# Four fused transformer layers on one core: the order of layer 0's first loads and keys, and unread products on constants in TensorE's waits

## The chip, the core and the metric

One core of a Trainium2 chip runs the whole program in one launch. The metric is device time in microseconds (us). Five engines work side by side, each through its own instructions in program order: TensorE (PE in the profile, with its weight loads as PEld), VectorE (DVE), ScalarE (ACT), GpSimd (POOL) and SyncE (SP, which only issues DMAs here; ACT issues some too, shown as ACTq).

## The reference

`x` has 1024 tokens of 128 features (16 batches of 64), `ctx_1024` as many. Four layers follow each other, all in float32:

```python
x = x + L0_xattn(ctx, ln(x), ...)   # 16 heads of 64; keys and values: ln(ctx) and ln(ln(x)), 128 a batch
x = x + L0_ffn(ln(x), ...)          # int8 weights, SiLU, 512 wide
x = x + L1_xattn(ln(x), ctx, ...)
x = x + L1_ffn(...)                 # mixture of 8 experts, two iterations
x = x + L2_xattn(ln(x), ctx, ctx, ...)   # 16 heads of 8, causal
x = x + L2_ffn(ln(x), ...)          # quantises by the largest |x| and the largest |hidden| of ALL tokens
x = x + L3_xattn(ln(x), ctx, ctx, ...)   # 16 heads of 8, scores outside a window raised by 1
x = x + L3_ffn(ln(x), ...)          # top 2 of 8 experts
```

In layer 0, with `A = Wq Wk^T / 8` and `N = Wv Wo` made for each head, scores are `(l A) kv^T` and the output is a sum over heads of `(softmax kv) N`. In layer 2's FFN the two maxima over all tokens are barriers: nothing behind one starts before every token has passed it.

## The kernel before, in words

**Layer 0** goes through eight pairs of batch groups `q` (four batches each). For each `q`, `l0_load` issues two DMAs into one `kv_tok` tile, the context rows from SP and the x rows from ACT. `l0_inputs` normalises it: `bn_stats` and `bn_aggr` (L154, L155), POOL's power (L161), four `tensor_scalar` (L183), a multiplication and an addition by `gains` (L403, L404; on DVE for q = 0, on POOL otherwise), four transposes on PE (L408), ACT's copy to `kvT` (L409), and two splits into float32r parts: `latT_hi` (L213) and `latT_lo` (L218) of the latent half, `tokp` of the tokens. `l0_project` then makes `G` (the latents times `A`) for eight pairs of heads, six products of 128x256 each (L236), copied by ACT (L425), and `l0_unit` has the scores (L445), the softmax on DVE, ACT and POOL (L447 to L461), the transposes (L465), the products with the tokens (L236) and with `N` (L479). Two `kv_tok` buffers take turns, so the load for `q + 2` waits until all readers of `q` are done. `l0_products` makes `A` and `N` (L326); `take_A` splits `A` into `A_hi` (ACT, L364) and `A_lo` (DVE, L365).

Units of layer 0 are interleaved, and one step of the tasks in `K.behind` (the weights and groups of the following sublayers) goes with each of them. A planner then puts the instructions of every engine into a final order by its own estimate of times, so a small edit can move instructions far from it. `in_turn` gives it an order between two instructions without a semaphore; `tc.issue_after` does the same for a block.

The order on SP at the start, as the source has it: `kv_tok` for q = 0, `WqT`, `gains`, `WqT`, `kv_tok` for q = 1, `WvT`, the four tiles of `x` (one for each group of four batches, first read when layer 0 adds its output), `cols` (every bias and small vector as columns), and then the weights of later layers. `later_constants` makes `half_cols` (half of `cols`, DVE L299), which ACT's sigmoid `sw` (L663) reads.

**Layers 2 and 3** have heads of 8 features. `heads_tile` goes through 16 tiles (group g, tile t): POOL lays out the keys (`kb`), PE adds a mask and the scores (L1262, L1263), DVE subtracts the maximum (L1264, L1265), ACT takes the exponential (L1266), PE transposes (L1273), ACT copies (`hpT`, L1274), PE multiplies by the values (L1283), DVE divides (L1291, L1292). `WARM` and `WARM_END` set how many unread products `keep_warm` puts behind the transposes of a tile: the weights are `identb` (a bf16 identity), what streams is a constant mask, and the output bank is never read. Before, this happens on the last two tiles of layer 3 (2, 4 and 2 products), sixteen times at the first queries of layer 2, and three times in layer 3's FFN for the groups g >= 2. `l2_ffn_hidden` has the two barriers, each through `global_amax`: a reduction on DVE, one product on PE (L1342), a reduction (L1344), four short steps (L1326 to L1331), and then the rounding of the tokens (`codes`, L1356 to L1359). `heads_keys` makes layer 3's keys on PE (L1137) and copies them with ACT (`hk`, L1147); part of it stands around the barriers.

Of the kernel before, what the change touches and what calls it, by code (L numbers as in the profile page):

```python
# [4 lines left out]


# [3 lines left out]

# [14 lines left out]
ALU = mybir.AluOpType  # L25
AX = mybir.AxisListType

P = 128
NT = 16
NG = 4  # L30
GT = 4
# [3 lines left out]
S = 64  # L35
EPS = 1e-5
NEG = -1.0e30
# [19 lines left out]
NCOL = sum(n for _, n in COLS)  # L57
# [150 lines left out]
def split(K, pool, src, name, engine=None, bufs=None, after=None):  # L208

    nc = K.nc  # L210
    hi = pool.tile(list(src.shape), F32R, name=f"{name}_hi", bufs=bufs)
    lo = pool.tile(list(src.shape), F32R, name=f"{name}_lo", bufs=bufs)
    first = nc.scalar.copy(hi, src) if isinstance(K, Later) else nc.vector.tensor_copy(hi, src)  # L213
    if after:
        in_turn(K, [after, first])
    if not isinstance(K, Later):
        K.mark = first
    (engine or nc.gpsimd).tensor_tensor(lo, src, hi.bitcast(F32), ALU.subtract)  # L218
    return hi, lo


# [61 lines left out]
def constants(K, pool):  # L283

    nc = K.nc
    K.ident = pool.tile([P, P], F32, name="ident")
    make_identity(nc, K.ident)
    K.neghalf = pool.tile([P, 1], F32, name="neghalf")
    nc.vector.memset(K.neghalf, -0.5)


def later_constants(K, pool):
    nc = K.nc
    K.identb = pool.tile([P, P], BF16, name="identb")
    nc.vector.tensor_copy(K.identb, K.ident)
# [3 lines left out]
    nc.vector.tensor_scalar(K.half, K.cols, 0.5, None, ALU.mult)  # L299

    K.pair_mask = pool.tile([P, GT, P], BF16, name="pair_mask")
    nc.vector.memset(K.pair_mask, NEG)
    for b in range(2):
        nc.vector.memset(K.pair_mask[b * S : (b + 1) * S, :, b * S : (b + 1) * S], 0.0)
# [11 lines left out]
N_TAGS = "2n"  # L316


def l0_products(K, out, left, right, hf, tags=("s", "t")):


    ps = [bank(K, tag, [P, 4, P]) for tag in tags]
    for j in range(4):
        for r in range(2):
            rows = slice(r * S, (r + 1) * S)
            K.nc.tensor.matmul(ps[r][:, j, :], left[rows, 4 * hf + j, :], right[rows, 4 * hf + j, :], start=True, stop=True)  # L326
    for r in range(2):
        out(ps[r], hf, r)


def l0_xattn(K):


    nc, tc, ins = K.nc, K.tc, K.ins
    with (
        tc.tile_pool(name="l0x_w", bufs=1, reuse_waits="tile") as wp,
        tc.tile_pool(name="l0x_g", bufs=2, reuse_waits="tile") as gp,
        tc.tile_pool(name="l0x_t", bufs=L0_BUFS, reuse_waits="tile") as tp,
    ):
        C = SimpleNamespace(gp=gp, tp=tp, tok={}, keys={}, G={})  # L340

        C.A = tuple(wp.tile([P, 16, P], F32R, name=f"A_{n}") for n in ("hi", "lo"))
        C.N = wp.tile([P, 16, P], F32, name="N")
        with tc.tile_pool(name="first", bufs=1, side="right", reuse_waits="tile") as first:
            l0_load(K, C, 0)
            w = {n: first.tile([P, 8, P], F32, name=n) for n in ("WqT", "WkT", "WvT", "Wo")}
            from_dram = {n: ins[f"L0_xattn_{n}"].rearrange("(c p) d -> p c d", p=P) for n in w}
            half = [slice(4 * hf, 4 * hf + 4) for hf in range(2)]
            gains = wp.tile([P, 2, P], F32, name="gains")
            K.kv_gamma, K.kv_beta = gains[:, 0, :], gains[:, 1, :]  # L350
            for hf in range(2):
                nc.sync.dma_start(w["WqT"][:, half[hf], :], from_dram["WqT"][:, half[hf], :])
                nc.scalar.dma_start(w["WkT"][:, half[hf], :], from_dram["WkT"][:, half[hf], :])
                if hf == 0:
                    nc.sync.dma_start(gains, ins["gains"])
            l0_load(K, C, 1)
            nc.sync.dma_start(w["WvT"], from_dram["WvT"])
            nc.scalar.dma_start(w["Wo"], from_dram["Wo"])
            heads = lambda t, hf, r: t.rearrange("p (c r) d -> p r c d", r=2)[:, r, half[hf], :]

            def take_A(ps, hf, r):
                hi, lo = (heads(a, hf, r) for a in C.A)
                scale = 1.0 / math.sqrt(64.0)
                nc.scalar.activation(hi, ps, AF.Copy, scale=scale)  # L364
                nc.vector.scalar_tensor_tensor(lo, ps, scale, hi.bitcast(F32), ALU.mult, ALU.subtract)  # L365

            l0_inputs(K, C, 0)
            for hf in range(2):
                l0_products(K, take_A, w["WqT"], w["WkT"], hf)
                for n in range(4 * hf, 4 * hf + 4):  # L370
                    l0_project(K, C, 0, n, "gn"[n % 2])
            l0_inputs(K, C, 1)

            with tc.issue_after(K.projected.ins):
                for hf in range(2):
                    l0_products(K, lambda ps, hf, r: nc.scalar.copy(heads(C.N, hf, r), ps), w["WvT"], w["Wo"], hf, N_TAGS)
        for g in range(NG):
            K.x[g] = K.load(K.const, f"x{g}", [P, GT, P], K.tokens(ins["x"], g))
        K.cols = K.load(K.const, "cols", [P, NCOL], ins["cols"])
        mid_begin(K)  # L380
        units = [(q, t, hf, b) for q in range(8) for t in range(2) for hf in range(2) for b in range(2)]
        interleave(K, (Task(l0_unit(K, C, *u)) for u in units), L0_DEPTH, L0_LAG, L0_RATE)


def l0_load(K, C, q):
    tok = C.tok[q] = C.gp.tile([P, GT, P], F32, name="kv_tok")
    for rows, name, queue in ((slice(0, S), "ctx_1024", K.nc.sync), (slice(S, P), "x", K.nc.scalar)):
        batches = K.ins[name].rearrange("(b s) d -> s b d", s=S)
        queue.dma_start(tok[rows, :, :], batches[:, GT * q : GT * (q + 1), :])


def l0_inputs(K, C, q):

    nc, gp = K.nc, C.gp
    tok = C.tok[q]
    mv = ln_moments(K, gp, tok)
    rs = gp.tile([P, GT], F32, name="ln_rs")
    nc.vector.tensor_scalar(rs[0:S, :], mv[0:S, :, 1], EPS, None, ALU.add)
    nc.vector.tensor_scalar(rs[S:P, :], mv[S:P, :, 1], 1.0 + EPS, EPS * EPS, ALU.mult, ALU.add)
# [5 lines left out]
    kvT = gp.tile(full, F32, name="kvT", bufs=3)  # L405
    ps = bank(K, "1", full)
    for b in range(GT):
        nc.tensor.transpose(ps[:, b, :], tok[:, b, :], K.ident)  # L408
    nc.scalar.copy(kvT, ps)  # L409
    latp = split(K, gp, kvT[:, :, S : 2 * S], "latT", nc.vector)  # L410
    tokp = split(K, gp, tok, "tokp", bufs=3)
    C.keys[q] = (kvT, latp, tokp)

# [14 lines left out]
def l0_unit(K, C, q, t, hf, b):  # L428
# [5 lines left out]
    G = C.G[q]  # L434
    if n == 0 and q + 2 < 8:
        l0_load(K, C, q + 2)
    if n == 2 and q + 2 < 8:
        l0_inputs(K, C, q + 2)
    if (hf, b) == (0, 0):
# [602 lines left out]
LAST_ENDS = ((2, 4), (2, 4))  # L1042
LAST_TAGS = "scgt"
HEAD_BLOCKS = ("L2", "L3")
WARM = ((0, 0, 0, 0), (0, 0, 2, 4))
WARM_END = 2


def heads_constants(K, pool):
# [185 lines left out]
def heads_tile(K, C, g, t):  # L1235
# [32 lines left out]
    pT = C.pp.tile([P, 8, P], F32, name="hpT")  # L1268
    for n in range(2):
        ps = bank(K, TURN[C.i], [P, 4, P])  # L1270
        for j in range(4):
            h = n * 8 + 2 * j
            turn = nc.tensor.transpose(ps[:, j, :], e[:, h : h + 2, :].rearrange("p h k -> p (h k)"), K.ident)  # L1273
        nc.scalar.copy(pT[:, n * 4 : n * 4 + 4, :], ps)  # L1274
    yield
    warm = WARM[C.i][t] if g == NG - 1 else 0
    if warm:
        keep_warm(K, bank(K, "s", [P, 512]), warm, turn)
    po = bank(K, AV[C.i][t % len(AV[C.i])], [P, 8, 2, 9])
# [21 lines left out]

    tiles = slice(t + 1 - n, t + 1)
    xg = K.x[g][:, tiles, :]
    if warm and t == GT - 1:
# [27 lines left out]
    return sc, inv  # L1332


def global_amax(K, pool, per_group, name):

    nc = K.nc
    one = pool.tile([P, 1], F32, name=f"{name}_one")
    nc.vector.tensor_reduce(one, per_group, AX.X, ALU.max)

    ps = bank(K, "g", [P, P])
    nc.tensor.matmul(ps, one.to_broadcast([P, P]), K.ident, start=True, stop=True)  # L1342
    out = pool.tile([P, 1], F32, name=f"{name}_all")
    nc.vector.tensor_reduce(out, ps, AX.X, ALU.max)  # L1344
    return out
# [22 lines left out]
def keep_warm(K, ps, n, after=None):  # L1368

    cols = ps.shape[-1]  # L1370
    moving = K.masks[1].rearrange("p h k -> p (h k)") if len(K.masks[1].shape) == 3 else K.masks[1]
    for _ in range(n):
        step = K.nc.tensor.matmul(ps, K.identb, moving[:, :cols], start=True, stop=True)
        if after is not None:
# [57 lines left out]
def l2_ffn_hidden(K, gp):  # L1432
    nc, wp = K.nc, K.l2p

    amax = global_amax(K, wp, K.l2am, "x")
    for xg in K.x:
        K.l2bo_step = nc.gpsimd.tensor_tensor(xg, xg, K.l2bo.unsqueeze(1).to_broadcast([P, GT, P]), ALU.add)
    sc, inv = scales(K, wp, amax, 1, 32767, "x")
# [10 lines left out]
    for g in range(NG):  # L1449
# [14 lines left out]
            if n == 1 or c % 2:  # L1464
                nc.vector.tensor_reduce(am[:, 4 * g + c : 4 * g + c + 1], h[:, c + 1 - n : c + 1, :], AX.XY, ALU.max, apply_absolute_value=True)
        K.l2h.append(h)
    amax = global_amax(K, wp, am, "h")
    sc, K.l2inv = scales(K, wp, amax, 1, 32767, "h")
    load_table(K, wp, AF.Exp, amax)
    steps = []  # L1470
# [48 lines left out]
def l3_ffn(K, gp, tp, g, tiles, tags):  # L1519
# [219 lines left out]
```

## Time and profile before

| | us |
|---|---|
| median of 3 runs (906.65 to 907.55) | 907.39 |
| the profiled execution, its own time | 907.62 |
| its span, first to last instruction | 905.9 |
| PE busy (share of the span) | 821.4 (91%) |
| DVE busy | 732.4 (81%) |
| ACT busy | 563.0 (62%) |
| POOL busy | 328.3 (36%) |

The span lies 1.7 us below the execution's own time. A busy share is an average over stages: in the first 17.9 us PE is busy for 5.25 us, from 30 to 310 us for 272.72 of 280 us. PEclk is the TensorE clock that the throttle granted; its mean is 0.98. The times of PE's instructions in one place against another tell the same thing for each instruction.

### The profile page before, as it was taken

The numbers are of one execution on the slowest core, as the hardware profiler recorded it, in microseconds if no ns is written. First come the engines' busy times: TensorE is split into PE (matmuls) and PEld (weight loads), VectorE is DVE, ScalarE is ACT, GpSimd is POOL, SyncE is SP. The second block draws the span as 40 slices with busy tenths as digits, with TensorE's granted clock in tenths as the row PEclk, the third lists the DMA queues.
The fourth block names the chain that finished last, engine by engine and source line by source line (L and its number), as shares of the span: only waits on it lengthen the run. The fifth ranks groups of instructions, "written<-read, shape, count | busy, mean of one in ns | idle before, by whom it ended". The sixth has DMA issues, their size and how long they took to land.

```text
span 905.9 us, 15766 instructions
## 1 busy us (share of the span) xinstructions
PE 821.4 (91%) x5859; PEld 671.2 (74%) x5868; DVE 732.4 (81%) x1877; ACT 563.0 (62%) x1093; POOL 328.3 (36%) x300
## 2 busy tenths in 40 slices
PE   4999999999999988899999799898999779898995
PEld 3989989979988876787787688684676447566663
DVE  5879799798698687877678877789788778789878
ACT  3676685676676599587687768564544484345443
POOL 3764574343243251511040310015474303435342
PEclk9999999999999999999999999999999999899998
DMA  8312000000000000000000000000000000000000
GB/s 191 106 36 59 13 2 12 13 1 1 13 1 1 1 13 0 15 14 21 1 1 1 1 1 1 0 25 1 1 2 1 1 1 1 1 1 1 13 13 24
DMA packets 22670, 13.73 MB, mean 15 GB/s; under 512 B 3009, under 2 KB 21953, under 8 KB 22593
## 3 DMA queue, kind: packets, MB, share of 16 engines
q1 hardware_dynamic: 18320, 10.62, 4.3%
q10 hardware_dynamic: 4272, 2.10, 0.9%
q8 instruction: 46, 0.75, 0.3%
q14 instruction: 32, 0.25, 0.1%
HBM read 11.66 MB, written 1.05 MB: 14 GB/s over the span
## 4 chain that ended last, share of the span: by engine, by line
PE 50%; DVE 25%; ACT 15%; POOL 3%; issue 3%; DMA 2%; SPq 1%; ACTq 0%; DVEq 0%; POOLq 0%
PE c_ps L918 7%; PE g_ps L479 4%; PE s_ps L1263 4%; PE s_ps L445 4%; PE g_ps L236 4%; PE c_ps L236 3%; PE g_ps L1283 2%; PE c_ps L1273 2%; PE s_ps L236 2%; PE t_ps L465 2%; PE t_ps L236 2%; ACT L941 2%; DVE mh_lo L895 1%; ACT L936 1%; DVE m L893 1%
## 5 line engine op out<-in xcount | busy, mean ns | idle before, releaser
L461 POOL TENSOR_TENSOR e<-e,rs 128x512 f32<-128x512 f32 x64 | 67.0, 1058 | 91.7 <-DVE rs L460 52.8
L161 POOL TENSOR_TENSOR ln_rstd<-ln_rs,neghalf 128x4 f32<-128x4 f32 (+1 forms) x38 | 40.8, 1073 | 144.8 <-DVE ln_rs L169 137.5
L1249 POOL TENSOR_TENSOR kb<-hk,head 128x1024 f32<-128x1024 f32 x32 | 63.7, 1993 | 74.2 <-PE s_ps L1263 58.9
L445 PE MATMUL s_ps<-kvT,G 128*128 128x128 f32 x512 | 71.7, 277 | 0.5 <-DVE e L451 0.5
L1263 PE MATMUL s_ps<-kb,hq 128*128 128x512 f32 x128 | 67.3, 609 | 2.1 <-ACT hq L1232 1.9
L445 PEld LDWEIGHTS s_ps<-kvT,G 128*128 128x128 f32 x512 | 65.8, 192 | 4.1 <-DVE e L451 1.9
L918 PE MATMUL c_ps<-mh_hi,w2e_hi 128*128 128x512 f32 x160 | 61.8, 426 | 4.5 <-ACT be L936 2.7
L479 PE MATMUL g_ps<-N,Ct 128*128 128x128 f32 x512 | 62.1, 276 | 1.1 <-ACT G L425 0.7
L479 PEld LDWEIGHTS g_ps<-N,Ct 128*128 128x128 f32 x512 | 60.1, 192 | 2.5 <-ACT G L425 1.3
L1266 ACT ACTIVATE e<-e 128x1024 f32<-128x1024 f32 x32 | 34.0, 1061 | 40.6 <-DVE e L1265 38.1
L1264 DVE TENSOR_REDUCE nm<-s_ps 128x8 f32<-128x512 f32 x64 | 43.7, 683 | 16.0 <-PE s_ps L1263 15.6
L1274 ACT COPY hpT<-c_ps 128x512 f32<-128x512 f32 x64 | 35.1, 589 | 34.2 <-PE c_ps L1273 33.9
L469 DVE TENSOR_TENSOR pT_lo<-t_ps,pT_hi 128x512 fp32r<-128x512 f32 x64 | 43.4, 683 | 13.5 <-ACT pT_hi L468 11.3
L918 PE MATMUL c_ps<-mh_hi,w2e_lo 128*128 128x512 f32 x160 | 51.9, 401 | 0.0
L895 DVE TENSOR_TENSOR mh_lo<-m,mh_hi 128x1024 fp32r<-128x1024 f32 x32 | 40.4, 1263 | 13.9 <-ACT mh_hi L894 12.9
L473 ACT COPY Ct<-c_ps 128x512 f32<-128x512 f32 x64 | 38.4, 600 | 21.2 <-PE c_ps L236 16.4
L918 PE MATMUL c_ps<-mh_lo,w2e_hi 128*128 128x512 f32 x160 | 49.4, 404 | 0.5 <-DVE mh_lo L895 0.5
L425 ACT COPY G<-g_ps 128x512 f32<-128x512 f32 x60 | 35.9, 598 | 21.4 <-PE g_ps L236 18.0
L452 ACT ACTIVATE e<-e 128x512 f32<-128x512 f32 x56 | 35.4, 638 | 20.8 <-DVE e L451 20.5
L1283 PEld LDWEIGHTS g_ps<-hv,hpT 128*64 128x64 f32 x1024 | 33.5, 137 | 19.3 <-issue 7.4
L447 DVE TENSOR_REDUCE nm<-s_ps 128x4 f32<-128x512 f32 x64 | 42.9, 679 | 5.0 <-PE s_ps L445 4.7
L468 ACT CAST pT_hi<-t_ps 128x512 fp32r<-128x512 f32 x64 | 38.1, 598 | 13.3 <-PE t_ps L465 7.3
(524 smaller groups left out, 2651.8 us busy)
## 6 DMA issues: line engine op xcount, KB each, us to landing
kv_tok<-in_x ACTq DMA_DIRECT2D x8, 128.0 KB, 3.3
kv_tok<-in_ctx SPq DMA_DIRECT2D x8, 128.0 KB, 2.9
x<-in_x SPq DMA_DIRECT2D x4, 256.0 KB, 8.3
ctx<-in_ctx SPq DMA_DIRECT2D x4, 256.0 KB, 3.4
w2e_raw<-in_L_ffn_expert_w SPq DMA_DIRECT2D x1, 768.0 KB, 4.4
out<-x SPq DMA_DIRECT2D x3, 256.0 KB, 2.3
WkT<-in_L_xattn_WkT ACTq DMA_DIRECT2D x2, 256.0 KB, 5.3
WqT<-in_L_xattn_WqT SPq DMA_DIRECT2D x2, 256.0 KB, 5.2
```

Source lines behind the costliest of these rows:

```text
L236: step = K.nc.tensor.matmul(ps, w[a], x[b], start=start and i == 0, stop=stop and i == 2)
L445: nc.tensor.matmul(ps[:, j, :], G[:, bb, h : h + 2, :].rearrange("p h s -> p (h s)"), kvT[:, bb, :], start=True, stop=True)
L447: K.mark = nc.vector.tensor_reduce(nm, ps, AX.X, ALU.max, negate=True)
L461: nc.gpsimd.tensor_tensor(e, e, rs.unsqueeze(2).to_broadcast([P, 4, P]), ALU.mult)
L469: nc.vector.tensor_tensor(lo, ps, hi.bitcast(F32), ALU.subtract)
L479: nc.tensor.matmul(ps, Ct[:, h, :], C.N[:, h, :], start=(h == 0), stop=(h == 15))
L895: nc.vector.tensor_tensor(lo, m, hi.bitcast(F32), ALU.subtract)
L918: nc.tensor.matmul(ps, K.w2p[part][:, 2 * n + i, cols], x[:, i, :, :], start=first, stop=last)
L1249: step = nc.gpsimd.tensor_tensor(kb, K.hk[C.i][g][:, :, t, :].unsqueeze(2).to_broadcast(full), K.head.unsqueeze(1).unsqueeze(3).to_broadca ...
L1263: nc.tensor.matmul(ps, hq[:, half, t, :, :].rearrange("p b s -> p (b s)"), kb[:, half, :, :], start=False, stop=True)
L1264: nc.vector.tensor_reduce(nm[:, heads], ps, AX.X, ALU.max, negate=True)
L1283: values = nc.tensor.matmul(po[b * S : (b + 1) * S, j, :, :].rearrange("p r d -> p (r d)"), pT[:, j, b * S : (b + 1) * S], K.hv[g][:, 2 * ...
```

## The change

At the start: `identb` and `pair_mask` are made first, eight unread products on them stand ahead of everything on PE, and six more behind the first half of `A`'s products. The second half of these products comes behind the transposes of q = 0. On DVE, the moments of q = 1 and `half_cols` come behind `latT_lo` of q = 0. On SP, `cols` moves ahead of `WvT`, and the four tiles of `x` move behind both loads for q = 2; the x rows of q = 2 are issued by SP in place of ACT. In the heads: unread products on the last two tiles of layer 2 (2, 4 and 2), on the first two of layer 3 (3 each), six ahead of the transposes of tile (2, 2) of layer 3, and three in layer 3's FFN of g = 1 as well. At the barriers: twelve behind the first maximum's product and five behind the second's. `keep_warm` streams `pair_mask` in place of layer 3's mask.

```diff
@@ split
-    (engine or nc.gpsimd).tensor_tensor(lo, src, hi.bitcast(F32), ALU.subtract)
+    K.split_end = (engine or nc.gpsimd).tensor_tensor(lo, src, hi.bitcast(F32), ALU.subtract)
@@ constants: identb and pair_mask are made here, no longer in later_constants
...
@@ later_constants
-    nc.vector.tensor_scalar(K.half, K.cols, 0.5, None, ALU.mult)
+    in_turn(K, [K.lat0, nc.vector.tensor_scalar(K.half, K.cols, 0.5, None, ALU.mult)])
@@ l0_products: with after=..., each product in_turn behind it
...
@@ l0_xattn
             l0_load(K, C, 0)
+            keep_warm(K, bank(K, "1", [P, 512]), WARM_START)
...
             l0_load(K, C, 1)
+            K.cols = K.load(K.const, "cols", [P, NCOL], ins["cols"])
             nc.sync.dma_start(w["WvT"], from_dram["WvT"])
...
+            step = l0_products(K, take_A, w["WqT"], w["WkT"], 0)
+            keep_warm(K, bank(K, "g", [P, 512]), 6, step)
             l0_inputs(K, C, 0)
             for hf in range(2):
-                l0_products(K, take_A, w["WqT"], w["WkT"], hf)
+                if hf:
+                    l0_products(K, take_A, w["WqT"], w["WkT"], hf, after=K.turn0)
...
-        for g in range(NG):
-            K.x[g] = K.load(K.const, f"x{g}", [P, GT, P], K.tokens(ins["x"], g))
-        K.cols = K.load(K.const, "cols", [P, NCOL], ins["cols"])
@@ l0_load
-        queue.dma_start(tok[rows, :, :], batches[:, GT * q : GT * (q + 1), :])
+        K.tok_step = (queue if q != 2 else K.nc.sync).dma_start(tok[rows, :, :], batches[:, GT * q : GT * (q + 1), :])
@@ l0_inputs
-    mv = ln_moments(K, gp, tok)
+    with K.tc.issue_after(K.lat0.ins) if q == 1 else nullcontext():
+        mv = ln_moments(K, gp, tok)
...
+    if q == 0:
+        K.turn0, K.lat0 = turn, K.split_end
@@ l0_unit
         l0_load(K, C, q + 2)
+        if q == 0:
+            for g in range(NG):
+                x = K.x[g] = K.const.tile([P, GT, P], F32, name=f"x{g}")
+                in_turn(K, [K.tok_step, K.nc.sync.dma_start(x, K.tokens(K.ins["x"], g))])
@@ heads
-WARM = ((0, 0, 0, 0), (0, 0, 2, 4))
+WARM = {(0, 3, 2): 2, (0, 3, 3): 4, (1, 0, 0): 3, (1, 0, 1): 3, (1, 3, 2): 2, (1, 3, 3): 4}
 WARM_END = 2
+WARM_TURN = {(1, 2, 2): 6}
+WARM_START = 8
@@ heads_tile
+        if n == 0:
+            keep_warm(K, ps.rearrange("p j k -> p (j k)"), WARM_TURN.get((C.i, g, t), 0))
...
-    warm = WARM[C.i][t] if g == NG - 1 else 0
+    warm = WARM.get((C.i, g, t), 0)
@@ global_amax
-    nc.tensor.matmul(ps, one.to_broadcast([P, P]), K.ident, start=True, stop=True)
+    step = nc.tensor.matmul(ps, one.to_broadcast([P, P]), K.ident, start=True, stop=True)
+    if warm:
+        keep_warm(K, bank(K, "s", [P, 512]), warm, step)
@@ keep_warm
-    moving = K.masks[1].rearrange("p h k -> p (h k)") if len(K.masks[1].shape) == 3 else K.masks[1]
+    moving = K.pair_mask.rearrange("p t k -> p (t k)")
@@ l2_ffn_hidden
-    amax = global_amax(K, wp, K.l2am, "x")
+    amax = global_amax(K, wp, K.l2am, "x", 12)
...
-    amax = global_amax(K, wp, am, "h")
+    amax = global_amax(K, wp, am, "h", 5)
@@ l3_ffn
-    if tiles.stop == GT and g >= NG - 2:
+    if tiles.stop == GT and g >= 1:
         keep_warm(K, ps[:, 64:512], 3, turn)
```

The planner's new order differs from the old one on all engines through layer 0 and around the barriers and in the heads; in between, in layer 1, it is the same.

More of the change, by code (lines that the diff above doesn't have):

```diff
@@ L7 @@
 import math
-from contextlib import ExitStack
+from contextlib import ExitStack, nullcontext
 from types import SimpleNamespace
@@ L287, in constants @@
     make_identity(nc, K.ident)
+    K.identb = pool.tile([P, P], BF16, name="identb")
+    nc.vector.tensor_copy(K.identb, K.ident)
+    K.pair_mask = pool.tile([P, GT, P], BF16, name="pair_mask")
+    nc.vector.memset(K.pair_mask, NEG)
+    for b in range(2):
+        nc.vector.memset(K.pair_mask[b * S : (b + 1) * S, :, b * S : (b + 1) * S], 0.0)
     K.neghalf = pool.tile([P, 1], F32, name="neghalf")
@@ L293, in later_constants @@
     nc = K.nc
-    K.identb = pool.tile([P, P], BF16, name="identb")
-    nc.vector.tensor_copy(K.identb, K.ident)
     K.identr = pool.tile([P, P], F32R, name="identr")
@@ L298, in later_constants @@
     K.half = pool.tile([P, NCOL], F32, name="half_cols")
[L299 to L304, printed above, removed]
+    in_turn(K, [K.lat0, nc.vector.tensor_scalar(K.half, K.cols, 0.5, None, ALU.mult)])
     K.rank = pool.tile([P, 8], F32, name="rank")
@@ L316, with l0_products @@
 N_TAGS = "2n"
-def l0_products(K, out, left, right, hf, tags=("s", "t")):
+def l0_products(K, out, left, right, hf, tags=("s", "t"), after=None):
     ps = [bank(K, tag, [P, 4, P]) for tag in tags]
@@ L325, in l0_products @@
             rows = slice(r * S, (r + 1) * S)
-            K.nc.tensor.matmul(ps[r][:, j, :], left[rows, 4 * hf + j, :], right[rows, 4 * hf + j, :], start=True, stop=True)
+            step = K.nc.tensor.matmul(ps[r][:, j, :], left[rows, 4 * hf + j, :], right[rows, 4 * hf + j, :], start=True, stop=True)
+            if after is not None:
+                in_turn(K, [after, step])
     for r in range(2):
         out(ps[r], hf, r)
+    return step
 def l0_xattn(K):
@@ L407, in l0_inputs @@
     for b in range(GT):
-        nc.tensor.transpose(ps[:, b, :], tok[:, b, :], K.ident)
+        turn = nc.tensor.transpose(ps[:, b, :], tok[:, b, :], K.ident)
     nc.scalar.copy(kvT, ps)
     latp = split(K, gp, kvT[:, :, S : 2 * S], "latT", nc.vector)
+    if q == 0:
+        K.turn0, K.lat0 = turn, K.split_end
     tokp = split(K, gp, tok, "tokp", bufs=3)
@@ L1303, in heads_tile @@
     xg = K.x[g][:, tiles, :]
-    if warm and t == GT - 1:
+    if warm and (g, t) == (NG - 1, GT - 1):
         keep_warm(K, bank(K, "s", [P, 512]), WARM_END, values)
@@ L1332, in scales, with global_amax @@
     return sc, inv
-def global_amax(K, pool, per_group, name):
+def global_amax(K, pool, per_group, name, warm=0):
     nc = K.nc
```

## The prediction

> **What bounds the kernel now.** I read the page first: span, busy shares, granted clock, the chain that ended last.
>
> ```profile
> span 905.9 us, 15766 instructions
> PE 821.4 (91%) x5859; PEld 671.2 (74%) x5868; DVE 732.4 (81%) x1877; ACT 563.0 (62%) x1093; POOL 328.3 (36%) x300
> ...
> PEclk9999999999999999999999999999999999899998
> ...
> PE 50%; DVE 25%; ACT 15%; POOL 3%; issue 3%; DMA 2%; SPq 1%; ACTq 0%; DVEq 0%; POOLq 0%
> ```
>
> PE is busy and on the chain for half the span, so the stages where it is not matter. Stretches of the span (length, busy times of PE, PEld, DVE, ACT, POOL, clock, DMA share, GB/s) find them:
>
> ```profile
> 0.00:17.90 17.90, 5.25 (x36) 4.35 (x36) 9.78 (x47) 6.03 (x8) 5.90 (x11) 1.00 0.93 219
> 30.00:310.00 280.00, 272.72 (x2118) 252.52 (x2119) 235.82 (x622) 186.41 (x393) 129.19 (x116) 1.00 0.07 20
> 722.00:725.40 3.40, 0.00 (x0) 0.00 (x0) 3.37 (x5) 2.42 (x4) 3.18 (x2) 1.00 0.00 0
> 725.50:728.80 3.30, 2.60 (x10) 2.13 (x12) 3.11 (x9) 1.17 (x2) 0.00 (x0) 0.50 0.00 0
> 776.70:780.00 3.30, 2.12 (x41) 1.88 (x41) 3.30 (x6) 1.32 (x3) 2.62 (x2) 1.00 0.00 0
> 780.10:786.90 6.80, 5.63 (x13) 3.09 (x13) 4.69 (x9) 1.37 (x2) 1.78 (x2) 0.50 0.00 0
> ```
>
> PE hardly works for 17.9 us, then waits only 7.3 us in 280 of layer 0: time won at the start should last. The 0.50 rows are stretches at half clock behind PE's waits. The timeline of the opening (start, duration, engine, line, instruction, idle time before it and its releaser) shows what holds PE back:
>
> ```profile
> 6.30 6.50 SPq L1593 DMA_DIRECT2D x<-in_x  x4
> 8.55 0.69 DVE L403 TENSOR_TENSOR kv_tok<-kv_tok,gains 128x512 f32<-128x512 f32 x1
> 12.17 0.87 DVE L154 BATCH_NORM_STATS2 ln_st<-kv_tok 128x6 f32<-128x128 f32 x4 [2.93 <-DMA kv_tok<-in_ctx]
> 12.84 0.83 SPq L1593 DMA_DIRECT2D cols<-in_cols  x1
> 12.96 0.67 DVE L404 TENSOR_TENSOR kv_tok<-kv_tok,gains 128x512 f32<-128x512 f32 x1
> 17.50 0.19 DVE L299 TENSOR_SCALAR half_cols<-cols 128x49 f32<-128x49 f32 x1 [0.51 <-DMA cols<-in_cols]
> 17.61 0.28 DVE L213 CAST latT_hi<-kvT 128x256 fp32r<-128x256 f32 x1
> 17.95 0.58 PE L236 MATMUL g_ps<-latT_hi,A_hi 128*128 128x256 f32 x1 [3.13 <-DVE latT_hi L213]
> ```
>
> The first keys wait twice for transfers that they don't need: L404 behind q = 1's moments, `latT_hi` behind `half_cols`. The clock is the third thing. The page shows it as full from the start, but PE's timeline doesn't:
>
> ```profile
> 23.66 1.06 PE L408 MATMUL c_ps<-ident,kv_tok 128*128 128x128 f32 x4
> 25.38 0.41 PE L236 MATMUL n_ps<-latT_hi,A_lo 128*128 128x256 f32 x1
> ...
> 27.98 0.27 PE L236 MATMUL g_ps<-latT_hi,A_lo 128*128 128x256 f32 x1
> ...
> 31.00 0.66 PE L408 MATMUL c_ps<-ident,kv_tok 128*128 128x128 f32 x4
> ```
>
> The same instructions start every 0.21 us up to about 25.7 and every 0.12 after it: the opening runs at half speed, 1.00 there being only the lack of a record.
>
> **The opening, step by step.** The sum is made against the profiled execution, 907.62 us (0.2 above the median). DVE's q = 0 chain: L183 ends at 8.51, L403 at 9.24, L404 directly behind it at 9.9 (was 13.6). PE: the eight products start once `identb` is there (3.4). One costs 0.42 at half clock (mask product at 783.36, next at 783.78) and 0.22 at full (768.98 to 769.20), so they end at 6.9; `A`'s first half takes 2.1 (6.42 to 8.50), to 9.0; six products 1.3 to 2.6; transposes 0.5 to 0.9; `A`'s second half 1.05 to 2.1. Before, the clock rose after 7.8 us of nearly full work (18 to 25.7: 7.40 of 7.70). PE is now full from 3.45, so a rise between 6.9 and 13.7 puts the first projection at 11.5 to 14.6. I take 12.5 (rise near 10.3), 5.4 earlier; `latT_lo`, through ACT's copy (0.6), 0.3 and 0.4 on DVE, is there at 12.9.
>
> Next come three serial queues. ACT's G copies stand behind `sw`, so behind `half_cols`, so behind `cols`: issued about 7 us earlier it lands near 10, in time. DVE's last `A_lo` (0.66) stands behind the moments of q = 2 (0.87), whose loads stand on SP behind `w_r`, `w_h`, `bs` (4.4 us of issuing) and `WvT`'s landing (13.7 before). Landing is 14.6 to 18.1; I take 16.8, so `A_lo` is ready at 18.4 and the fifth projection, at 27.43 before, runs near 18.5: 8.9 earlier. POOL then has two powers, four `gains` steps of 1.3, `tokp_lo` 1.27 and the first `e` 1.05 in one row: from 18.7 (second pair waiting for L183, 20.9) to 28.5. The first transposes of `e`, at 36.30 before, start there: 7.8 earlier. **Lead: 8** (bounds 0, if one of these queues is later than any row shows, and 9.5).
>
> SP: the four loads of `x` (6.50 of issuing) go behind q = 2's loads and ahead of `bs`, `wf` and q = 3's, which waits anyway until `tokp_lo` of q = 1 has freed its buffer (25.59 before, about 27.4 now); `x` is first read after 50 us. Zero. The memsets and `identb` stood in DVE's first 3.4 us already; `pair_mask` in place of a mask of the same shape: zero.
>
> **Layer 0's order.** The planner has moved instructions on every engine through layer 0. PE's waits there are 7.3; I take no change, bounds minus 3 to plus 20 (the PE share of 200 to 210 us, 8.92 of 10, throughout would be 30).
>
> **First barrier.** Twelve products (2.6) follow the product at 720.64, in a wait that lasts until 725.98 with no PE work from 722.0. They leave 2.3 of idle time. If that keeps the clock, the eight transposes take 1.04 as at 730.04 and not 1.97, and the chain to ACT's Gelu gains 1.0 (bounds minus 0.2, one key product now standing ahead of the maximum's, to 1.2). I take 1.0.
>
> **Second barrier.** Five products (1.1) fit into PE's 2.02 wait before 745.48, but the last key product comes behind them, so its copy on ACT (0.95 at 745.61) moves behind the scaling of the hidden layer. That scaling is the chain there (L1476 2.56, L1481 4.99): 0.9 won, 0.15 lost at 745.48 (bounds minus 0.3 to 0.95).
>
> **Heads.** In the start of layer 3, six products go into tiles 0 and 1; the second three fall into the 0.62 wait at 778. The cold stretch behind it costs 0.85 a score pair twice (1.91 for 1.02) and 0.65 on transposes, 2.4 in all. The 1.83 idle before 781.27 stays, so I take half: 1.2 (0 to 2.4).
>
> The Trainium skill, "TensorE: Matmul & The Clock Gate", section "Why this matters for your kernels", says that only idle gaps above about 3 us throttle the clock: by it these six are worth nothing and the forecast is 1.2 later. The rows decide: with 2.12 of 3.30 us busy the clock still fell to 0.50.
>
> The six ahead of tile (2, 2) land near 828, too early for the cold stretch at 838: nothing won; 1.3 of PE in front of transposes whose `e` was ready at 826.1, of which DVE's own wait there (0.68) covers half: 0.65 lost (0 to 1.3). Layer 2's eight and the three in g = 1 lie in waits for ACT of 0.67 and more (713.75, 842.33); if that cover goes, 2.4 at most. I take 0.15.
>
> **Sum:** 8.0 + 1.0 + 0.75 + 1.2 - 0.65 - 0.15 = 10.15; 907.62 - 10.15 = 897.5, and 897.3 at the median's level.
>
> **Rivals.**
> - *Half a lead.* A queue (q = 2's landing ahead of `A_lo`, POOL's row) holds the first softmax until 32: lead 4, 901.3. For it: DVE and POOL become serial just there. Against: every step has its row.
> - *The products keep no clock.* The 54 don't raise the clock before 13.7, nor at the barrier or in layer 3: lead 7, barrier two's 0.75, minus 0.8: 900.5. For it: 780 fell at 64% busy. Against: the rise at 25.7 after full work.
> - *Everything holds.* Lead 9.5, all 2.4 at 780, no product in front of ready work: 907.4 - (9.5 + 1.0 + 0.9 + 2.4) = 893.6.
> - *Slower: layer 0's new order.* DVE is busy for 235.82 of 280 us (84%), and PE has two banks each for scores and transposes; a wrong order on DVE stalls PE at once. PE's waits would have to grow from 7.3 to over 19.3 in 280 us to make it slower by more than 0.2%; at 22 it is 912. Against: the old order lost 2.6%.
>
> **How the numbers follow.** Forecast 0.50, half a lead 0.19, no clock kept 0.15, everything 0.08, slower 0.08. 892.5 to 903.5 takes in the bounds of all but the last and leaves out about 0.16. About 0.2% (1.8 us) is what a measurement can tell from no change. Faster: the first four cases less their tail, 0.88; same 0.04; slower 0.08.
>
> **What would show it.** L404 at 9.9 and the first projection near 12.5; PE's L236 every 0.12 us from its first; the first transposes of `e` near 28.5; PE waits near 7 in 280 us of layer 0; clock 1.00 behind the first barrier; ACT's scaling directly behind the table load. A first projection after 15, or more than 12 us of PE waits in layer 0, would prove me wrong.

## The result: 0.3% slower, and the profile after

The changed kernel takes 909.99 us (median of 13 executions, 906.02 to 912.62); the kernel before took 907.02 beside it (13 executions). The ratio is 1.0032, 95% interval 1.0018 to 1.0046: a loss of 3 us where a gain of 10 was forecast. The executions of one kernel lie up to 11 us apart, and the mean granted clock mostly goes with them (in `both_no_turn_g2` below 896.10 us at 0.986, 907.00 at 0.972), so medians and ratios decide, and a trace is one execution. The profiled one took 910.61 us. Its page, the lines shown of before:

```profile
span 908.9 us, 15877 instructions
PE 830.9 (91%) x5909; PEld 674.1 (74%) x5922; DVE 737.0 (81%) x1877; ACT 563.4 (62%) x1093; POOL 328.1 (36%) x300
...
PEclk9999999999999999999999999999999999999899
...
PE 47%; DVE 28%; ACT 15%; issue 4%; POOL 3%; DMA 2%; SPq 0%; DVEq 0%; ACTq 0%; POOLq 0%
```

DVE's share of the chain rises from 25% to 28%: it has become more of a bound. Stretches of after, columns as before:

```profile
0.00:17.90 17.90, 13.48 (x93) 9.12 (x94) 9.36 (x45) 8.95 (x14) 4.78 (x10) 1.00 0.77 169
18.00:25.70 7.70, 5.23 (x30) 4.78 (x29) 6.04 (x23) 1.17 (x2) 3.62 (x4) 0.78 0.59 170
30.00:310.00 280.00, 268.44 (x2069) 246.84 (x2068) 240.81 (x621) 182.48 (x376) 129.43 (x117) 1.00 0.07 21
726.00:728.70 2.70, 0.62 (x3) 0.10 (x1) 2.70 (x5) 0.30 (x2) 1.94 (x1) 1.00 0.00 0
839.80:846.60 6.80, 6.05 (x18) 3.82 (x19) 2.95 (x7) 3.63 (x6) 0.00 (x0) 0.50 0.15 41
```

The first 17.9 us are what the change wanted: PE works for 13.48 instead of 5.25. Then PE waits (18 to 25.7: 5.23 of 7.70, where before it had 7.40), the clock falls again, and in layer 0 PE's waits grow from 7.3 to 11.6. At the first barrier (726) the twelve products leave 2.1 us without work, near the 2.3 that were forecast, and the clock falls all the same, at 730.55 for 3.41 us. The last row comes back below. In the chain of waits of after the opening hangs on q = 2's loads:

```profile
7.91 6.50 DMA WvT<-in_L_xattn_WvT
14.42 0.50 SPq L697
15.05 0.60 SPq L394
15.69 3.44 DMA kv_tok<-in_x
19.22 0.87 DVE ln_st L154 x4
20.09 0.59 DVE A_lo L370
```

and the timeline shows who stands behind it (in this kernel L370 is `A_lo`, L410 and L411 apply the gains, L405 and L406 make `ln_rs`, L479 has the transposes of `e`):

```profile
9.18 0.69 DVE L411 TENSOR_TENSOR kv_tok<-kv_tok,gains 128x512 f32<-128x512 f32 x1
11.98 0.36 PE L236 MATMUL g_ps<-latT_hi,A_hi 128*128 128x256 f32 x1 [0.18 <-PE t_ps L326]
19.22 0.87 DVE L154 BATCH_NORM_STATS2 ln_st<-kv_tok 128x6 f32<-128x128 f32 x4 [5.18 <-DMA kv_tok<-in_x]
20.01 0.67 DVE L370 SCALAR_TENSOR_TENSOR A_lo<-t_ps,A_hi 128x512 fp32r<-128x512 f32 x1
20.74 0.58 PE L236 MATMUL g_ps<-latT_hi,A_lo 128*128 128x256 f32 x1 [2.47 <-DVE A_lo L370]
21.01 1.99 POOL L161 TENSOR_TENSOR ln_rstd<-ln_rs,neghalf 128x4 f32<-128x4 f32 x2 [9.33 <-DVE ln_rs L406]
32.89 0.60 PE L479 MATMUL t_ps<-ident,e 128*128 128x128 f32 x4
```

The first projection is 6 us earlier than before, the first transposes of `e` only 3.4. Of those nothing is left at the end of layer 0, and the place is visible on DVE and POOL:

```profile
42.91 2.04 POOL L475 TENSOR_TENSOR e<-e,rs 128x512 f32<-128x512 f32 x2 [0.83 <-PE g_ps L236]
43.92 4.08 DVE L183 TENSOR_SCALAR kv_tok<-kv_tok,ln_mv,ln_rstd 128x128 f32<-128x128 f32 x4
45.03 2.38 POOL L218 TENSOR_TENSOR w1e_lo<-w1e_raw,w1e_hi 128x1024 fp32r<-128x1024 f32 x1
48.09 1.28 DVE L406 TENSOR_SCALAR ln_rs<-ln_mv 64x4 f32<-64x4 f32 x1
53.81 2.22 DVE L183 TENSOR_SCALAR kv_tok<-kv_tok,ln_mv,ln_rstd 128x128 f32<-128x128 f32 x4
```

The rows of before for the first transposes of `e`, the same L183 and `w1e_lo`:

```profile
36.30 0.66 PE L465 MATMUL t_ps<-ident,e 128*128 128x128 f32 x4
41.92 1.11 DVE L183 TENSOR_SCALAR kv_tok<-kv_tok,ln_mv,ln_rstd 128x128 f32<-128x128 f32 x4
48.47 2.39 POOL L218 TENSOR_TENSOR w1e_lo<-w1e_raw,w1e_hi 128x1024 fp32r<-128x1024 f32 x1 [0.67 <-ACT w1e_hi L213]
```

Four L183 took 1.11 before, and `w1e_lo` came 5 us behind them. In after they take 4.08: DVE is shown as busy, but the first two last until `w1e_lo` on POOL is done (45.03 + 2.38 = 47.41). L406, on 64x4, takes 1.28 for its usual 0.17. The busy columns hide a wait. The table below cuts both traces at the same instructions. Scores are counted by DVE's maxima of them (`nm<-s_ps`): 64 in layer 0, then two for each tile of layers 2 and 3. Score 88 is the first of tile (3, 0) of layer 2, 96 the first of layer 3, 112 and 120 the first of its groups 2 and 3.

| stretch, after less before in us | forecast | measured |
|---|---|---|
| to the first transposes of `e` (36.30, 32.89) | -7.8 | -3.4 |
| from there to the last product with `N` (319.61, 321.89) | 0 | +5.7 |
| from there to score 88 | 0 | +0.4 |
| scores 88 to 96: both barriers | -1.75 | -0.8 |
| scores 96 to 104: start of layer 3 | -1.2 | -2.05 |
| scores 104 to 112 | 0 | 0 |
| scores 112 to 120: group 2, with tile (2, 2) | +0.65 | +2.9 |
| 120 to the end | +0.15 | +0.3 |

### The profile page after: what moved, and what is told of

Its sections match the earlier page's. It is cut to its first block, busy times and chain, and to the rows that moved or that the text cites. A ratio compares the mean times of both kernels' runs of the same rounds, so it can differ in the third digit from the quotient of the medians.

```text
span 908.9 us, 15877 instructions
## 1 busy us (share of the span) xinstructions
PE 830.9 (91%) x5909; PEld 674.1 (74%) x5922; DVE 737.0 (81%) x1877; ACT 563.4 (62%) x1093; POOL 328.1 (36%) x300
## 4 chain that ended last, share of the span: by engine, by line
PE 47%; DVE 28%; ACT 15%; issue 4%; POOL 3%; DMA 2%; SPq 0%; DVEq 0%; ACTq 0%; POOLq 0%
PE c_ps L932 6%; PE s_ps L1279 4%; PE g_ps L493 4%; PE s_ps L459 4%; PE c_ps L236 3%; PE g_ps L236 3%; PE c_ps L1291 2%; PE s_ps L236 2%; PE g_ps L1301 2%; PE t_ps L236 2%; PE t_ps L479 2%; ACT L955 2%; DVE nm L1280 2%; DVE e L1281 1%; DVE kv_tok L183 1%
## 5 line engine op out<-in xcount | busy, mean ns | idle before, releaser
L1292 ACT COPY hpT<-c_ps 128x512 f32<-128x512 f32 x64 | 35.1, 588 | 35.8 <-PE c_ps L1291 35.6
L483 DVE TENSOR_TENSOR pT_lo<-t_ps,pT_hi 128x512 fp32r<-128x512 f32 x64 | 43.3, 680 | 15.9 <-ACT pT_hi L482 13.7
L461 DVE TENSOR_REDUCE nm<-s_ps 128x4 f32<-128x512 f32 x64 | 42.9, 678 | 4.6 <-PE s_ps L459 4.4
```

The lines of the kernel that those rows point to most:

```text
L461: K.mark = nc.vector.tensor_reduce(nm, ps, AX.X, ALU.max, negate=True)
L483: nc.vector.tensor_tensor(lo, ps, hi.bitcast(F32), ALU.subtract)
```

## The experiments

Each edit is against the changed kernel where nothing else is said. The table has the median in us of 6 to 13 executions, the ratio to before on the same chip (whose median was 906.4 to 907.1) with its 95% interval, and from the one trace of each run the first transposes of `e`, the time from there to the last product with `N`, and three of the stretches above.

| run | median | ratio (interval) | first `e` | to end of layer 0 | 88-96 | 96-104 | 112-120 |
|---|---|---|---|---|---|---|---|
| before | 907.0 | 1 | 36.3 | 283.3 | 70.9 | 23.3 | 33.9 |
| after | 910.0 | 1.0032 (1.0018-1.0046) | 32.9 | 289.0 | 70.1 | 21.2 | 36.8 |
| open_only | 908.6 | 1.0025 (1.0010-1.0039) | 32.6 | 290.0 | 70.0 | 23.3 | 33.8 |
| q2_behind | 901.8 | 0.9929 (0.9904-0.9954) | 28.9 | 281.9 | 68.1 | 21.2 | 36.7 |
| q2_first | 906.0 | 0.9996 (0.9979-1.0013) | 28.8 | 288.7 | 68.7 | 21.2 | 36.9 |
| q2_no_start | 905.8 | 0.9989 (0.9976-1.0002) | 34.1 | 283.3 | 68.7 | 21.2 | 36.8 |
| after_no_low | 902.8 | 0.9954 (0.9938-0.9969) | 32.0 | 285.0 | 69.0 | 21.2 | 36.9 |
| before_no_low | 908.0 | 1.0004 (0.9985-1.0022) | 36.1 | 283.3 | 70.2 | 21.8 | 35.8 |
| first_late | 903.9 | 0.9963 (0.9951-0.9975) | 30.2 | 285.9 | 68.1 | 21.2 | 36.7 |
| heads_only | 907.4 | 1.0008 (0.9994-1.0023) | 37.4 | 283.0 | 68.1 | 21.2 | 36.6 |
| heads_no_turn | 906.0 | 0.9999 (0.9980-1.0017) | 37.3 | 282.5 | 68.1 | 21.2 | 35.8 |
| no_turn | 909.5 | 1.0025 (1.0007-1.0043) | 32.0 | 288.5 | 68.7 | 21.2 | 33.9 |
| q2_open_only | 898.8 | 0.9926 (0.9899-0.9953) | 28.4 | 281.9 | 71.0 | 23.3 | 33.9 |
| q2_no_turn | 898.0 | 0.9909 (0.9889-0.9928) | 28.2 | 281.8 | 68.1 | 21.2 | 35.8 |
| both | 901.8 | 0.9940 (0.9917-0.9963) | 30.0 | 282.0 | 70.2 | 21.2 | 36.8 |
| both_no_turn | 897.1 | 0.9874 (0.9855-0.9894) | 29.9 | 282.0 | 69.7 | 21.2 | 33.9 |
| both_no_turn_g2 | 896.7 | 0.9902 (0.9867-0.9937) | 27.3 | 281.9 | 68.1 | 21.2 | 35.8 |

**The opening alone, and the heads alone.** `open_only` gives the heads and barriers back their old products; `heads_only` is before with the new ones.

```diff
-WARM = {(0, 3, 2): 2, (0, 3, 3): 4, (1, 0, 0): 3, (1, 0, 1): 3, (1, 3, 2): 2, (1, 3, 3): 4}
-WARM_TURN = {(1, 2, 2): 6}
+WARM = {(1, 3, 2): 2, (1, 3, 3): 4}
+WARM_TURN = {}
...
-    if tiles.stop == GT and g >= 1:
+    if tiles.stop == GT and g >= NG - 2:
```

(and `global_amax` without the 12 and the 5.) Expected of `open_only`:

> The opening's part of the change alone: the heads and the barriers are as before, the first loads, the first keys and the 14 products on constants at the start are as after. Theory (the opening's lead is gone by 90 us and layer 0 ends 2.3 us later than before, everything behind it only shifted): 909.3 us, 1.0025 of the time before; layer 0's last product with N 2.3 us later than before; the cold stretches near 726 and 780 us are back. Rival (the loss of 3.0 us was made in the heads, and layer 0's 2.3 is caught up behind it in layer 1's waits): 907.0.

and of `heads_only`:

> The products in the heads and at the two barriers alone; the opening and layer 0 are as before. Theory (from the two traces: 1.0 won over the two barriers, 2 to 2.9 won at the start of layer 3, 3.0 lost from 833 to 847 us): 907.4 us, within 0.1% of before. Rival (where the clock falls depends on the moment at which the heads are reached, not on the products, so 2.3 us earlier the loss at 833 is not there): 904.5.

Both theories held: 1.0025 and 1.0008. The loss is the opening's; the products of the heads and barriers, for which 2.15 us were forecast, are in sum not to be told from nothing (interval -0.0006 to +0.0023).

**q = 2's moments off the queue.** `q2_behind` changes the order on DVE only:

```diff
-        mv = ln_moments(K, gp, tok)
+        mv = ln_moments(K, gp, tok, after=(K.apply1, K.a_lo) if q == 2 else ())
```

(`apply1` is the last L183 of q = 1, `a_lo` the last `A_lo`; each `bn_stats` stands `in_turn` behind both.)

> The changed kernel with the moments of q = 2 on VectorE put behind the last step of A_lo and the four normalising steps of q = 1. Theory one (the 5.2 us that VectorE waits at 14 us for the transfer of q = 2 is what cost the first keys their lead): A_lo ready near 15, no fall of the clock at 20.6, first transposes of e near 27 instead of 32.9, and 3 to 5 us of it kept at the end: 905 to 907. Theory two (from 40 to 60 us VectorE is the bound and waits inside its instructions for GpSimd, 5.7 us more than before, which takes any lead): transposes of e at 27 all the same, but the end within 1 us of after: 909 to 911.

In its timeline:

```profile
14.68 0.66 DVE L372 SCALAR_TENSOR_TENSOR A_lo<-t_ps,A_hi 128x512 fp32r<-128x512 f32 x1
19.54 0.87 DVE L154 BATCH_NORM_STATS2 ln_st<-kv_tok 128x6 f32<-128x128 f32 x4 [1.71 <-DMA kv_tok<-in_x]
```

901.8, 8.2 us under after. The landing is as late as in after, but `A_lo` no longer waits for it (14.68, L372 here). The clock is full from 7.6 us to the end of layer 0, and the first transposes of `e` stand at 28.9 (4.0 earlier; 27 was expected). A further 7.1 is won behind them, for the planner's new order also moved DVE's L183 away from `w1e_lo`: the four of q = 3 take 1.11 at 36.78, and `w1e_lo` stands at 41.77. The first theory holds for the 4.0; the rest needed the next runs.

**The transfer itself.** `q2_first` leaves DVE's order as it is and changes SP's:

```diff
+    if q == 2:
+        K.tok2 = step
...
-        (queue or nc.sync).dma_start(t, src)
+        behind_tok2(K, (queue or nc.sync).dma_start(t, src))   # in_turn behind tok2: w_r, w_h, bs
```

> The changed kernel with SyncE's queue alone changed: the loads for q = 2 (and with them those of x) ahead of the small loads w_r, w_h and bs; VectorE's order at the start is that of after. Theory (the landing of q = 2 at 19.2 is what held A_lo): landing near 15, VectorE's wait of 5.2 us down to about 1, A_lo near 16, no fall of the clock at 20.6, the first transposes of e 3 to 4 us earlier than in after (29 to 30); the end 3 to 4 us earlier, 906 to 907, if the later loss at 45 stays, and more if it goes. Rival (the order on VectorE, not the transfer): 909 to 910.

In the timeline of `q2_first` SP's issue of the x rows, DVE's wait, `A_lo`, the first `e` and L183 of q = 3 are to be held against after's:

```profile
11.89 0.62 SPq L394 DMA_DIRECT2D kv_tok<-in_x  x1
15.06 0.87 DVE L154 BATCH_NORM_STATS2 ln_st<-kv_tok 128x6 f32<-128x128 f32 x4 [0.82 <-DMA kv_tok<-in_x]
15.85 0.68 DVE L370 SCALAR_TENSOR_TENSOR A_lo<-t_ps,A_hi 128x512 fp32r<-128x512 f32 x1
28.75 0.60 PE L481 MATMUL t_ps<-ident,e 128*128 128x128 f32 x4
39.78 4.06 DVE L183 TENSOR_SCALAR kv_tok<-kv_tok,ln_mv,ln_rstd 128x128 f32<-128x128 f32 x4
```

The x rows land near 15, DVE waits 0.82 for 5.18, and everything to the first `e` comes 4.1 us earlier, L183's 4.06 included. The median falls by 4.0. So the landing cost 4 us, and the loss between 40 and 57 us is a second one that goes with the order, not with the time.

**The second loss.** `after_no_low` leaves two steps of POOL out, `w1e_lo` and `w2e_lo`:

```diff
-    return split(K, pool, raw, name, after=after)
+    return split(K, pool, raw, name, after=after, low=name not in ("w1e", "w2e"))   # low=False: hi, hi
```

> The changed kernel without GpSimd's two steps that make the low parts of layer 1's expert weights (w1e_lo, 128x1024, 2.4 us at 45; w2e_lo, 128x1536, 3.5 us at 57); the high part is read in their place, so TensorE's work is the same and layer 1's result is not that of the reference. Theory (VectorE's normalising steps wait inside their own time until GpSimd's step is done; that took 2 to 4 us of the lead between 47 and 73 us): L183 at 45 takes 0.3 us and not 2.5, the product with N number 48 stands 2 to 3 us earlier than in after (71.0 for 73.0), layer 0 ends 2 to 3 us earlier, in all 907 to 908. Rival (the order of PE's instructions took the lead): those products at the same place within 0.5 us, 910.

`before_no_low` does the same to before:

> The kernel before with the same two GpSimd steps left out as in after_no_low (low parts of layer 1's expert weights; the high part is read in their place, so layer 1's result is not the reference's). Theory (the two steps hurt only where they meet VectorE's normalising of q = 2 and 3, as the order of after has it; before, VectorE has no prolonged step between 43 and 60 us): within 1 us of before, 906 to 907. Rival (5.9 us less of GpSimd's work in layer 0 is worth the same anywhere): 900.

The L183 of q = 3 and 4 in `after_no_low`, for 4.08 and 2.22 in after:

```profile
43.05 1.88 DVE L183 TENSOR_SCALAR kv_tok<-kv_tok,ln_mv,ln_rstd 128x128 f32<-128x128 f32 x4
49.41 1.11 DVE L183 TENSOR_SCALAR kv_tok<-kv_tok,ln_mv,ln_rstd 128x128 f32<-128x128 f32 x4
```

From the first `e` to the end of layer 0 after falls from 289.0 to 285.0, which is 4.0 of the 5.7 lost; before stays at 283.3. So in layer 0 these steps cost nothing in the old order. (They meet the L183 of q = 3 and 4; the expectation of `before_no_low` counted one too low.) The other 1.7 is not traced to a step. The ratios, 0.9954 for 1.0032 of after, and 1.0004, say less: `after_no_low` fell by 7.2 us where 2 to 3 were expected, and 2.6 of that lies between layer 0 and score 88 in the traces; `before_no_low` had a lower granted clock than the executions of before beside it (median 0.972 for 0.980), so its ratio alone would not exclude a gain. `first_late` is `q2_first` with the two steps moved, nothing left out:

```diff
+    if name in ("w1e", "w2e"):
+        in_turn(K, [K.beta3, K.split_end])   # behind q = 3's addition of the gains on POOL
```

> q2_first with GpSimd's two steps for layer 1's weights (w1e_lo, w2e_lo) moved behind q = 3's last gain step on GpSimd; nothing is left out, VectorE's order is the same up to 50 us. Theory (it is where these steps stand, not that they are done: VectorE's L183 of q = 3 and 4 wait inside their time for them): L183 of q = 3 falls from 4.06 to 2 us or less, layer 0 ends 2 to 4 us earlier than in q2_first (314 to 315.5 for 317.5), the end at 902 to 904. Rival (it is GpSimd's 5.9 us of work, which holds the e steps at any place): 905.5 to 906.5.

Its timeline:

```profile
41.20 1.88 DVE L183 TENSOR_SCALAR kv_tok<-kv_tok,ln_mv,ln_rstd 128x128 f32<-128x128 f32 x4
47.56 3.17 DVE L183 TENSOR_SCALAR kv_tok<-kv_tok,ln_mv,ln_rstd 128x128 f32<-128x128 f32 x4
47.76 2.37 POOL L218 TENSOR_TENSOR w1e_lo<-w1e_raw,w1e_hi 128x1024 fp32r<-128x1024 f32 x1
```

q = 3's four fall from 4.06 to 1.88, but `w1e_lo` now meets q = 4's (3.17 for 2.23). The stretch still falls from 288.7 to 285.9 and the median by 2.2. So the place counts, and not the work alone. How much of it is DVE's hold and how much POOL's own queue (in `after_no_low` q = 3's addition ended 3 us earlier than in after) the runs don't separate.

**The 14 products at the start.** `q2_no_start` is `q2_behind` without them.

```diff
-WARM_START = 8
+WARM_START = 0
...
-            keep_warm(K, bank(K, "g", [P, 512]), 6, step)
+            keep_warm(K, bank(K, "g", [P, 512]), 0, step)
```

> q2_behind without the 14 products on constants at the start. Theory (they keep TensorE's clock in the opening: from 6.9 us it is full): the clock is half until some 20 us, the first projection near 14 and not 12.7, the first transposes of e 1 to 2 us later and the end 1 to 2 us later: 903.3. Rival (the queues of VectorE and GpSimd, not TensorE, set the first e, and the products only stand in front of the first half of A): the same end within 0.5 us, 901.8.

4.0 us slower, more than expected. The clock rises at 16.1 us (6.1 to 12.8 in twelve traces with the products). But the first projection is only 0.3 later and the first `e` 5.3, with another order of the planner on POOL and DVE behind it: clock and order are mixed in this number.

**The products in the heads.** `no_turn`, `q2_no_turn` and `heads_no_turn` take the six ahead of tile (2, 2) out of after, `q2_behind` and `heads_only`; `both` puts them back into `both_no_turn`:

```diff
-WARM_TURN = {(1, 2, 2): 6}
+WARM_TURN = {}
```

> The changed kernel without the six products ahead of the transposes of tile (2, 2) of layer 3. Theory (the six push that tile's scores behind the tokens' normalising on VectorE, which waits for GpSimd and takes 4.2 us, and PE's 2.6 us wait behind it drops the clock for 6.8 us): 3.0 us less than after, 907.0 us; the scores of (2, 3) ahead of the normalising again. Rival (the clock falls there anyway, by the grid of its windows): 909.5 to 910.

> q2_behind without the six products ahead of tile (2, 2) of layer 3. Theory (in every trace with the six, the stretch from the scores of tile 112 to those of 120 takes 36.6 to 36.8 us, and 33.8 to 33.9 without them): 2.8 us less than q2_behind, 899.0. Rival (no_turn won 0.5 in the median where its trace had won 2.8: behind it the clock falls at another place): 901.3.

> The kernel before with the products in the heads and at the barriers, but without the six ahead of tile (2, 2). Theory (by the traces the six cost 2.9, the barriers' 17 and the start of layer 3 win 1.9 and 2.05): 907.4 of heads_only less 2.9, 904.5. Rival (as no_turn against after, whose medians differ by 0.5 only): 907.

> both_no_turn with the six products ahead of tile (2, 2) put back. Theory (six products push the scores of that tile behind the tokens' normalising: by the traces 36.7 us from scores 112 to 120 for 33.8 to 35.8 without them): 1 to 3 us slower than both_no_turn, 899 to 900. Rival (no cost in the mean over executions, as no_turn against after): 897.

Removing them changed the ratios by 0.0007, 0.0020, 0.0009 and 0.0066 (0.6, 1.8, 0.8 and 6.0 us; the last pair ran on two chips, and its medians differ by 4.7), always the same way, though the first three within their intervals. `no_turn` came out at its rival's time, `heads_no_turn` between theory and rival, `q2_no_turn` 1 us below its theory and `both` 2 above it. In the traces the stretch from score 112 to 120 takes 36.6 to 36.9 with the six (8 traces) and 33.8 to 35.8 without (9): on average 2.0 us. In before's timeline and in after's:

```profile
830.58 1.02 PE L1263 MATMUL s_ps<-kb,hq 128*128 128x512 f32 x2
...
834.94 1.02 PE L1279 MATMUL s_ps<-kb,hq 128*128 128x512 f32 x2
834.99 4.21 DVE L183 TENSOR_SCALAR l_xn<-x,ln_mv,ln_rstd 128x128 f32<-128x128 f32 x4 [0.54 <-POOL ln_rstd L161]
836.95 1.90 POOL L1265 TENSOR_TENSOR kb<-hk,head 128x1024 f32<-128x1024 f32 x1
839.83 1.09 PE L1551 MATMUL g_ps<-ident,l_xn 128*128 128x128 f32 x4 [2.64 <-DVE ho L1310]
```

The scores, at 830.58 before, now follow the transposes at 834.94, so DVE takes the tokens' four L183 first; these wait for three POOL steps (4.21 us; 1.29 and 1.23 in `no_turn`), `ho` for them, PE for `ho` (2.64). The clock falls in that gap, but the six neither make nor prevent this: it falls at this place in all 17 traces. With the six it is at half for 6.83 us in all eight; without them for 3.41 in five (33.8 to 33.9 us for the stretch) and for 10.24 or 17.07 in four (35.8). So the rival was right about the fall, and the theory about the order: even against the longer falls the six cost 1.0 us.

`q2_open_only` is `q2_behind` without any of the new products behind layer 0 (the diff of `open_only`), `both_no_turn_g2` lacks the three of g = 1:

> The opening of after with the moments of q = 2 behind q = 1's normalising, and the heads and barriers as before, without their products. Theory (the products in the heads and at the barriers are worth nothing in sum, as heads_only with 907.4 for 907.1 has it): 901 to 902, the same as q2_behind within 1 us; 8.9 us won by the end of layer 0. Rival (heads_only's zero holds for one position only; 9 us earlier the products are worth the 2.15 that was forecast): 904.

> both_no_turn with the three products of layer 3's FFN for g = 1 taken out (g >= 2 only, as before). Theory (from scores 120 to the end the traces with them take 62.1 to 62.9 us and without them 61.8): 0.5 less, 896.6. Rival (they keep the clock behind 840 us): 898 to 899.

`q2_open_only` has 0.9926 for `q2_behind`'s 0.9929: no difference, as its theory says. The medians are 3.0 apart, but the executions of `q2_behind` lie in two groups (896.5 to 897.1 at a clock of 0.988 to 0.993, and 901.6 to 906.5 at 0.979 to 0.982). The three of g = 1 can't be told from nothing (0.9902 for 0.9874, intervals overlap).

What the other products are worth without the six is not settled. At the first barrier the clock fell in all four traces without the twelve and still in six of the thirteen with them, at the start of layer 3 in all four and in none of the thirteen. From score 88 to the end before, `open_only` and `q2_open_only` take 211.7 us (`before_no_low`, with 17 us at half clock, 215.2), the eight traces with all products 211.8 on average, the five without the six 209.6. But the ratios of `heads_no_turn` and before, `no_turn` and `open_only`, `q2_no_turn` and `q2_open_only` differ by 0.0001, 0.0000 and 0.0017, all within their intervals.

**Both repairs.** `both_no_turn` has `q2_behind`'s order on DVE, `q2_first`'s on SP, and no six products:

> The best of the runs so far (q2_no_turn: the changed kernel, moments of q = 2 behind q = 1's normalising, no products ahead of tile (2, 2)) with the loads for q = 2 ahead of w_r, w_h and bs on SyncE. Theory (the first scores of q = 0 on VectorE stand behind the moments of q = 2, which wait for the landing at 19.2): landing near 15, first transposes of e near 25 instead of 28.2, 2 to 3 us less at the end: 895.5. Rival (from 29 us on GpSimd and VectorE are the bound and take it): 898.

897.1, 0.9874 of before (0.9855 to 0.9894): the lowest ratio, 9 and 13 us under the medians of before and after; the intervals of `q2_no_turn` and `both_no_turn_g2` overlap with it. 895.5 was expected, with the first `e` near 25. Whether `q2_first` adds to `q2_no_turn` (898.0) is not settled: its traced execution got its clock at 12.8 us and the first `e` only at 29.9.

## Why the prediction was wrong, step by step

**Right.** L404's counterpart at 9.2 to 9.9, `cols` in time, the half clock of the opening (in `heads_only`, which has before's opening, a record shows 0.50 from 18.11 to 24.94), its rise in after (6.9), the first projection (11.98 for 12.5). The mechanism of the lead too: with `A_lo` out of the queue the first `e` came at 28.2 to 28.9 in three kernels where 28.5 was said, and the lead lasted through layer 0 (8.9 us at its end in `q2_behind`). That the number fits so well is luck: in `q2_behind` `A_lo` was ready at 15.3, 3.1 before the sum has it, and the way from there to the transposes took 13.6 us for 10.1. Neither of the two signs that were to prove the prediction wrong (a first projection after 15, over 12 us of waits in layer 0) came: they were the wrong signs.

**The step that failed first: "Landing is 14.6 to 18.1; I take 16.8".** It was 19.1. The chain's lines give the terms: `WvT` 14.42 (13.7 before), one `bs`, the context rows, then 3.44 for the x rows, which the change had put behind them on the same queue. With 2.3 us too little there, `A_lo`, `ln_rs` of q = 1 and all of POOL's row came later; "half a lead" had named this queue and priced it at 4, and 3.4 was measured at `e`. The way from POOL's first power to the transposes was also 11.9 long instead of 9.8: POOL's steps took their 9.6, but there were 1.4 of waits between them and 0.9 behind `e`.

**The step that failed worst: "Layer 0's order: I take no change".** It cost 5.7 us, 4.0 of them with `w1e_lo` and `w2e_lo`, which cost layer 0 nothing in the old order. The rival for a slower kernel had the engine (DVE, 84% busy, in a wrong order) but looked for it in PE's waits above 19.3 us; 11.6 sufficed, since the lead was smaller than assumed and the heads won nothing. The rows of before had not been searched for L183's spread: there four take 1.11 at 41.92, but one alone takes 1.06 at 91.17, beside a step of POOL. That was the warning. The mean of L183 on `kv_tok` in the first 90 us is 424 ns before and 589 after, for the same 20.

**The heads.** Taken by their own stretches, the barriers' 1.75 were right in size: 68.7 us on average in 13 traces with the products, 70.5 in 4 without (after's own trace shows 0.8). For the second barrier the prediction reads a wait of 2.02 before 745.48; the row of before has 1.20. The start of layer 3 was undersized: 2.05 for 1.2 (0.6 against the trace of `before_no_low`, where the cold stretch was short anyway). The six at (2, 2) were undersized: 0.65 was their own time less a cover, and their push to the order of DVE was put at nothing; 1.0 to 2.9 was measured. That these stretches add up to a gain at the end is not shown.

**Where the second mechanism stands.** The Trainium skill's page "SBUF — State Buffer", section "Who interferes with whom", says that VectorE's copies, casts and `tensor_scalar` on SBUF data may use a port pair that it shares with GpSimd, and that whoever comes second waits until the other's instruction is done. The rows agree: L183, L406 and the casts (`tokp_hi` 1.48 at 27.92 for 0.43) are just these forms. The long ones last until a POOL step beside them has ended, or up to 0.3 us more, while a reduction from PSUM beside POOL keeps its 0.68 (L461 at 43.33). Without the two POOL steps the same L183 are short again (`after_no_low`).

## What to carry to other kernels

A step moved ahead of a transfer pays only if nothing else on its engine waits for another transfer in between: follow the queue of every engine that the moved step crosses, with the landing worked out term by term. An engine's busy time can hold waits: compare the duration of the same instruction across the trace, and where VectorE's SBUF-to-SBUF steps are longer than their shortest, look at GpSimd beside them before a planner's new order is counted as neutral. Unread products belong only where PE's queue is empty behind them as well; one that delays a score can cost more time than it saves.

## What the runs showed of the hardware

- Up to 880 us the 17 traces have 113 falls to half clock; all stretches last 3.41 us or a multiple. 111 of the falls came behind a 3.41 us stretch in which PE worked for 65% or less; but at 45% to 65% the clock was often kept as well (139 stretches). The place of the stretches differs between executions: around the same instructions `no_turn` has 3.41 us at half clock and `heads_no_turn` 10.24. "TensorE: Matmul & The Clock Gate" of the Trainium skill, "Part 1: The HAM clock gate (the "warmup" mystery)", says the windows run freely and that the same kernel differs by their phase; these traces agree. Its rule of 3 us idle gaps, weighed in the prediction, is too lax here: the wait at 840 was 2.64.
- Two falls came without idle time. Stretches of `q2_behind`, columns as above:

```profile
861.00:864.40 3.40, 3.29 (x21) 2.30 (x21) 1.41 (x4) 0.59 (x1) 0.00 (x0) 0.99 0.29 82
864.40:874.60 10.20, 10.20 (x82) 7.67 (x83) 6.67 (x31) 1.62 (x6) 2.25 (x3) 0.50 0.00 0
```

PE is shown at work without a gap and still has half the clock for 10.2 us. `first_late` shows the same at 869.0. In both, 12 products of only eight columns each (the gates of layer 3's FFN, one every 0.11 us) fill a good part of the stretch ahead, at the same place in it; 30 other stretches with 12 of them kept the clock. Whether such small products count as little work is not tested, and the cause stays open.
